# Where the lists' padding rows are written: whole regions early, or 128 rows behind each list's end

## The chip, the cores and the metric

The kernel runs on one core of a Trainium2 chip. A core has a matrix engine (TensorE, PE in the profile), a vector engine (VectorE, DVE), a scalar engine (ScalarE, ACT), GpSimd (POOL) and a sync engine (SP), each with its own in-order instruction stream; they meet through semaphores. Sixteen DMA engines move data between DRAM and the on-chip memory (SBUF). The DMAs of this kernel are issued by the sync engine, two small ones by ScalarE, and the scatters by GpSimd. The metric is the device time of one execution in microseconds, the median of several runs.

## What is computed

One block of a transformer on x of shape (4, 512, 512): a cross-attention whose output is added through a gate, and then a mixture of experts, added through a second gate. Both read x after a layer norm. Cut to what matters:

```python
x = x + tanh(g_xattn) * attention(layernorm(x), ctx, Wq, Wkv, Wout)   # 16 heads, 64 keys, causal
xf = layernorm(x).reshape(2048, 512)
scores = softmax(xf @ gate_w.T)                  # 8 experts
weights, idx = top_k(scores, 2)                  # two experts for every token
g = silu(xf @ w1[e].T) * (xf @ w3[e].T)          # every expert e, 512 -> 256
eo[e] = g @ w2[e].T                              # 256 -> 512
y = sum over the token's two experts of weight * eo[e]
z = silu(xf @ ws1.T) * (xf @ ws3.T) @ ws2.T      # a shared expert, for every token
out = x + tanh(g_ffn) * (y + z)
```

All is in float32. An expert sees only the tokens that chose it.

## The kernel before

**Stages.** The four batches go through attention one after another (`attention()`, L631). In the turn of batch b, TensorE also does what is left of batch b - 1: its output projection, the second layer norm's transposes, the gate product (`gate`, L378), the sum of the gate's parts (L390), and `choose` (L408), which picks two experts for each token on VectorE. The turn after that has `route` (L451) for that batch: two small products (L455 and L458) give each token its rank in its expert's list, `places()` turns ranks into row numbers on VectorE, and `scatter(t)` has GpSimd write 128 rows by an indirect DMA (L474), two for each of four tiles. The last batch has its own function, `last_routing` (L790), in which products of the shared expert (L622) fill TensorE's time.

**The lists.** `xg_d` is a tensor in DRAM with a region for each of eight experts, `CAP` = 2048 rows each, and a tail of seven tiles of 128 rows. A row is 528 floats: 512 of the token, and 16 that say where its result goes and with which weights. A list is filled from the start of its region. The experts' products read it in tiles of 128 rows, and the last tile of a list is only partly filled; a row that no token wrote must hold zeros and the number of a spare result row. So the kernel writes such a row (`zeros`, in SBUF, L249) over all of `xg_d` at the start: eight DMAs of 16 tiles and one of seven, L251 to L256, on the sync engine's queue, behind the loads of the inputs. A tenth DMA (L257) clears the results `y_d`. The first scatter waits for all nine.

`zeros` is the end of the tile `gs_sb`, into which the shared expert's products of the last batch are written late in the kernel; so those writes wait for every DMA that reads `zeros`.

**GpSimd's stream.** Its order is written by hand. In each turn it scales the softmax (`softmax`, L338, two instructions), then runs the eight scatters of `route`, prepares the tails of the rows (L510, L511), and scales the second half of the softmax. TensorE transposes that second half (L345) behind the gate product.

**After the last batch.** `tile_table` (L527) counts each list with one product (L530), and VectorE makes from the counts the row, the expert and the rank of each of up to 39 tiles (`row_of`, `expert_of`, `rank_of`, L544 to L581). Then comes the loop over tiles: `fetch(j)` (L858) on the sync engine reads the row number into a register (L862), and issues four DMAs of 64 KB (L864) and one small one (L870); VectorE transposes the tile in blocks (L885); TensorE multiplies by w1 and w3 (L897), by an identity (L916) and by w2 (L924); GpSimd adds the result into `y_d` by two indirect DMAs (L931). Fetches run four tiles ahead. In the end `y_d` is read back, added to the shared expert's output (L958) and to x, and stored.

**Who sets the order.** From L826 the order of TensorE, GpSimd, VectorE and ScalarE follows the program text by hand; the sync engine's is set by a scheduler with its own estimate of the times. Its queue before has, in this order: input loads, the nine fills, the clearing of `y_d`, the shared expert's weights (L588), w1 and w3 of all experts (L832), w2 of all experts (L839, eight loads), and the fetches. The first two blocked transposes of fetched tiles (L947) lie outside the hand-written part, so the scheduler places them on VectorE.

Of the kernel before, what the change touches and what calls it, by code (L numbers as in the profile page):

```python
# [14 lines left out]
I32 = mybir.dt.int32  # L15
AF = mybir.ActivationFunctionType
ALU = mybir.AluOpType
AX = mybir.AxisListType

P = 128  # L20
B, S, D = 4, 512, 512
SK, L = 64, 128
NH, HD = 16, 32
NE, FF = 8, 256
DC = D // P
QT = S // P
NT = B * QT
# [2 lines left out]
NPAIR = NH // 2  # L30
TOPK = 2
CAP = B * S

MAXT = (TOPK * B * S + NE * (P - 1)) // P
MINT = TOPK * B * S // P
ROWS = NE * CAP + (MAXT - TOPK * B * S // P) * P


META = 16
ROW = D + META  # L40
# [7 lines left out]
def gated_cross_attention_moe(  # L48
# [14 lines left out]
    nc = tc.nc  # L63
    const = ctx.enter_context(tc.tile_pool(name="const", bufs=1))
# [13 lines left out]
    zeros = gs_sb[:, B * FC * S - ROW :].unsqueeze(1)  # L78
# [16 lines left out]
    xg_d = dram.tile([ROWS, ROW], F32, name="xg_d")  # L95
    y_d = dram.tile([2 * (B * S + P), YH], F32, name="y_d")
    y_rows = y_d.rearrange("(r h) d -> r (h d)", h=2)
    xg_w = dram_disjoint_views(xg_d, TOPK * NT)
    y_w = dram_disjoint_views(y_d, 2)

    ident = const.tile([P, P], F32, name="ident")
# [6 lines left out]
    for c in range(1, DC):  # L108
# [4 lines left out]
        out=before, in_=ones, compare_op=ALU.is_gt, fill=0.0,  # L113
# [5 lines left out]
    for j in range(2):  # L119
# [8 lines left out]
        out=mask[:, 0, 0, :], in_=mask[:, 0, 0, :], compare_op=ALU.is_ge, fill=NEG,  # L128
# [5 lines left out]
    def counting(name, shape, pattern, base=0):  # L134
        n = int(np.prod(shape))
        i = const.tile([P, n], I32, name=f"{name}_i")
        nc.gpsimd.iota(i, pattern=pattern, base=base, channel_multiplier=0)
        f = const.tile([P, *shape], F32, name=name)
        counts.append((f.rearrange("p a b -> p (a b)"), i))
        return f  # L140
# [5 lines left out]
        channel_multiplier=2,  # L146
    )
    rank = counting("rank", [1, NE], [[-1, NE]], base=NE)
    region = counting("region", [1, NE], [[CAP, NE]])
    tile_start = counting("tile_start", [1, CAP // P], [[P, CAP // P]])  # L150
    tile_no = counting("tile_no", [MAXT, 1], [[1, MAXT]])

# [60 lines left out]
    with ExitStack() as attn:  # L213
# [22 lines left out]
        for b in range(1, B):  # L236
            nc.sync.dma_start(
                out=xs[b], in_=x[ts(b, S), :].rearrange("(t p) d -> p t d", p=P)
            )

        for g in range(HC):
            for j in range(2):
                nc.sync.dma_start(
                    out=wo_sb[ts(g, HD), j::2, :], in_=wo[ts(2 * (g % 2) + j, HD), g // 2 :: 2, :]
# [3 lines left out]

        nc.gpsimd.memset(zeros, 0.0)  # L249
        nc.gpsimd.tensor_copy(zeros[:, 0, D : D + 2].bitcast(I32), token[:, NT, :])  # L250
        for lo in range(0, ROWS, CAP):  # L251
            n = min(CAP, ROWS - lo) // P
            nc.sync.dma_start(  # L253
                out=xg_d[lo : lo + n * P, :].rearrange("(n p) d -> p n d", p=P),
                in_=zeros.broadcast_to([P, n, ROW]),
            )  # L256
        nc.sync.dma_start(  # L257
            out=y_rows.rearrange("(n p) d -> p n d", p=P),
            in_=zeros[:, :, 0:D].broadcast_to([P, NT + 1, D]),
# [191 lines left out]
        def route(b, xn, des, hot, hot2, both, earlier):  # L451

            pr = ps_mm.tile(full, F32, tag="mm", name="pr")
            flat = "p t e -> p (t e)"
            nc.tensor.matmul(  # L455
                pr.rearrange(flat), before, both.rearrange(flat), start=True, stop=False
            )
            nc.tensor.matmul(  # L458
                pr.rearrange(flat), ones, earlier.rearrange(flat), start=False, stop=True
            )  # L460

            def places():
                place = wide("place")
                nc.vector.tensor_tensor(place, pr, region.broadcast_to(full), ALU.add)
                for k, h in enumerate((hot, hot2)):
                    at = wide(f"at{k}")
                    nc.vector.tensor_tensor(at, place, h, ALU.mult)
                    where = row(at, ALU.add, f"where{k}")
                    nc.vector.tensor_copy(pos[b][:, :, k : k + 1], where)

            def scatter(t):
                nc.gpsimd.tensor_copy(xn[t][:, D + 2 : D + 5], des[:, t, :])
                for k in range(TOPK):
                    nc.gpsimd.indirect_dma_start(  # L474
                        out=xg_w[TOPK * (b * QT + t) + k],
                        out_offset=IndirectOffsetOnAxis(ap=pos[b][:, t, k : k + 1], axis=0),
                        in_=xn[t], in_offset=None,
                    )

            return places, scatter  # L480
# [43 lines left out]
                [xr.tile([P, ROW], F32, tag="xn2", name="xn2", bufs=QT) for t in range(QT)], b  # L524
            )

        def tile_table():  # L527

            pn = ps_mm.tile([P, 1, NE], F32, tag="mm", name="pn")
            nc.tensor.matmul(pn[:, 0, :], ones, taken[B], start=True, stop=True)  # L530
            n = small.tile([P, NE, 1], F32, tag="n", name="n")
            nc.vector.tensor_copy(n[:, :, 0], pn[:, 0, :])

            def table(shape, name):
                return const.tile([P, *shape], F32, name=name)

            def summed(src, shape, name):
                r = table(shape, name)
                nc.vector.tensor_reduce(r, src, AX.X, ALU.add)
                return r  # L540

            full = [P, NE, CAP // P]
            starts = table(full[1:], "starts")
            nc.vector.tensor_tensor(  # L544
                starts, n.broadcast_to(full), tile_start.broadcast_to(full), ALU.is_gt
            )
            tiles = table([1, NE], "tiles")
            nc.vector.tensor_reduce(tiles[:, 0, :], starts, AX.X, ALU.add)
            ends = table([1, NE], "ends")
            nc.vector.tensor_copy(ends, tiles)  # L550
            for e in range(1, NE):
                nc.vector.tensor_tensor(
                    ends[:, :, e : e + 1], ends[:, :, e - 1 : e], tiles[:, :, e : e + 1], ALU.add
                )
            full = [P, MAXT, NE]
            over = table(full[1:], "over")
            nc.vector.tensor_tensor(
                over, ends.broadcast_to(full), tile_no.broadcast_to(full), ALU.is_le
            )
            expert = summed(over, [MAXT, 1], "expert")  # L560
            nc.vector.tensor_tensor(over, over, tiles.broadcast_to(full), ALU.mult)
            first = summed(over, [MAXT, 1], "first")
            rows = table([MAXT, 1], "rows")
            nc.vector.tensor_tensor(rows, tile_no, first, ALU.subtract)
            nc.vector.tensor_scalar(rows, rows, float(P), None, ALU.mult)
            nc.vector.scalar_tensor_tensor(rows, expert, float(CAP), rows, ALU.mult, ALU.add)
            row_of = const.tile([P, MAXT], I32, name="row_of")
            nc.vector.tensor_copy(row_of, rows[:, :, 0])
            nc.vector.tensor_scalar(expert, expert, float(NE - 1), None, ALU.min)
            expert_of = const.tile([P, MAXT], I32, name="expert_of")  # L570
            nc.vector.tensor_copy(expert_of, expert[:, :, 0])


            rank_of = const.tile([P, MAXT], F32, name="rank_of")
            nc.vector.tensor_scalar(
                rank_of, expert[:, :, 0], -1.0, float(NE), ALU.mult, ALU.add
            )


            more = const.tile([P, 1], I32, name="more")  # L580
            nc.vector.tensor_scalar(more, ends[:, 0, NE - 1 :], -float(MINT), None, ALU.add)  # L581
            return row_of, expert_of, rank_of, more
# [207 lines left out]
        def last_routing(at, chosen, parts):  # L790
            ps_f = ending.enter_context(tc.tile_pool(name="ps_f", bufs=2, space=PSUM))
            filling = shared_in_turn(parts, ps_f)

            def fill(n):
                for _ in range(n):
                    next(filling)

            def scatter_all(places, scatter):
                places()
                for t in range(QT):  # L800
                    scatter(t)

            b = B - 1
            xn2 = addressed([rows_sb[:, ts(t, ROW)] for t in range(QT)], b)
            mv, rstd = new_stats()
            for t in range(QT):
                project_out(b, at, t)
                if not t:
                    scatter_all(*route(b - 1, *chosen))
                moments(b, mv, t)  # L810
            deviation(mv, rstd)()
            second_rows_of(xn2, b, mv, rstd)
            fill(5)
            turn(xn2, x2t[b])
            fill(1)
            scored = gate(b)
            fill(1)
            chosen = choose(b, gate_sum(scored))
            fill(6)
            scatter_all(*route(b, xn2, *chosen))  # L820
            table = tile_table()
            for _ in filling:
                pass
            return table
# [278 lines left out]
```

## Time and profile before

| | us |
|---|---|
| median of 3 runs | 469.99 (467.15 to 470.5) |
| profiled execution, its own time | 469.66 |
| its span | 467.9 |
| TensorE busy | 452.7 (97%) |
| VectorE busy | 253.1 (54%) |
| GpSimd busy | 178.9 (38%) |
| ScalarE busy | 131.1 (28%) |

98.10 MB go through the DMA engines, of which 62.71 MB are written to DRAM; the nine fills of `xg_d` are eight of 4224 KB and one of 1848 KB.

How to read it: a busy time is a sum over stages with different limits, and a share near 100% doesn't say that all of it is useful. "L338" is line 338 of the kernel. "pr<-pr,rs" is what an instruction writes and what it reads. "SPq" and "POOLq" are the instruction queues of the sync engine and GpSimd. The clock of TensorE (PEclk) is what the chip grants, as a share of full speed. A time in the trace is counted from the start of the span.

### The profile page before, as it was taken

What the parts mean: (1) busy time and instruction counts of PE and PEld (TensorE: products, weight loads), DVE (VectorE), ACT (ScalarE), POOL (GpSimd) and SP (SyncE); (2) the same over time, 40 slices, a digit from 0 to 9 for tenths busy, and PEclk for the clock granted to TensorE, in tenths of its full rate; (3) what the DMA queues carried; (4) which work ended last, traced back from release to release, by engine and by line L of the source; (5) the groups of instructions that cost most, each with busy time, mean ns of one, the idle gap of its engine ahead of it and who ended that gap; (6) DMA issues with size and microseconds to landing.
All of it is one profiled execution on the core that took longest, in us unless ns stands there. A gap on an engine that the chain in (4) does not pass through costs nothing.

```text
span 467.9 us, 6177 instructions
## 1 busy us (share of the span) xinstructions
PE 452.7 (97%) x1718; PEld 232.7 (50%) x1718; DVE 253.1 (54%) x604; ACT 131.1 (28%) x245; POOL 178.9 (38%) x188
## 2 busy tenths in 40 slices
PE   6999999999989999999999999999999999999994
PEld 5875555564646465454444444444444444444332
DVE  5659698779905975656421344333343333342485
ACT  3357642762533255413011111111111111111000
POOL 3003321303280374251600555565556565555400
PEclk9999999999997999999999999999999999999998
DMA  8989999999992040799835575666665666544498
GB/s 264 317 305 385 387 385 387 386 387 385 400 340 55 1 164 23 272 406 418 352 75 130 106 122 91 98 101 107 95 101 91 97 105 105 79 50 51 55 376 335
DMA packets 70783, 98.10 MB, mean 210 GB/s; under 512 B 11728, under 2 KB 40144, under 8 KB 69584
## 3 DMA queue, kind: packets, MB, share of 16 engines
q1 hardware_dynamic: 58096, 80.01, 50.9%
q0 software_dynamic: 12352, 17.57, 20.8%
q8 instruction: 17, 0.28, 0.3%
q14 instruction: 30, 0.25, 0.2%
q10 hardware_dynamic: 288, 0.00, 0.0%
HBM read 34.84 MB, written 62.71 MB: 208 GB/s over the span
## 4 chain that ended last, share of the span: by engine, by line
PE 65%; SPq 17%; DMA 7%; issue 4%; DVE 3%; POOL 2%; ACT 0%; DVEq 0%; POOLq 0%
PE ph L897 25%; SPq L253 16%; PE py L924 12%; PE ph L622 6%; PE pd L370 6%; PE ph L596 4%; DMA xg_d<-gs_sb 4%; PE pz L958 3%; DMA wo_sb<-in_wo_dram 2%; POOL xg_d L474 2%; PE pg L916 2%; PE early L596 1%; DVE yk L1028 1%; PE po L359 1%; DVE yk L1047 1%
## 5 line engine op out<-in xcount | busy, mean ns | idle before, releaser
L931 POOL DMA_INDIRECT y_d<-y,meta x68 | 105.6, 1553 | 103.2 <-DVE y L928 60.8
L897 PE MATMUL ph<-w_all,xgt 128*128 x272 | 122.5, 593 | 0.1
L897 PEld LDWEIGHTS ph<-w_all,xgt 128*128 128x128 f32 x272 | 49.1, 190 | 49.6 <-issue 49.5
L338 POOL TENSOR_TENSOR pr<-pr,rs 128x1024 f32<-128x1024 f32 x16 | 30.3, 1903 | 110.5 <-DVE rs L337 94.7
L924 PE MATMUL py<-w_all,gt 128*128 x136 | 63.9, 592 | 0.0
L908 DVE SCALAR_TENSOR_TENSOR g<-sl,w,ph 128x256 f32<-128x256 f32 x34 | 16.3, 481 | 87.4 <-ACT sl L906 87.4
L292 PE MATMUL pq<-xt,wq_sb 128*128 128x512 f32 (+1 forms) x160 | 56.9, 511 | 2.5 <-ACT xt L198 1.6
L370 PE MATMUL pd<-wo_sb,at 128*128 128x512 f32 x128 | 56.1, 595 | 0.0
L906 ACT ACTIVATE sl<-ph 128x256 f32<-128x256 f32 x34 | 13.1, 384 | 109.0 <-PE ph L897 109.0
L292 PEld LDWEIGHTS pq<-xt,wq_sb 128*128 128x128 f32 x160 | 29.7, 190 | 26.4 <-issue 20.1
L924 PEld LDWEIGHTS py<-w_all,gt 128*128 128x128 f32 x136 | 25.8, 190 | 32.5 <-issue 32.5
L928 DVE COPY y<-py 128x512 f32<-128x512 f32 x34 | 23.5, 692 | 27.8 <-PE py L924 27.8
L370 PEld LDWEIGHTS pd<-wo_sb,at 128*128 128x128 f32 x128 | 23.9, 190 | 29.1 <-issue 27.7
L958 PE MATMUL pz<-sh,gs_sb 128*128 128x512 f32 (+1 forms) x68 | 28.1, 570 | 1.4 <-DVE y L928 0.9
L622 PE MATMUL ph<-x2t,sh 128*128 128x512 f32 x64 | 28.6, 596 | 0.0
L918 ACT COPY gt<-pg 128x256 f32<-128x256 f32 x34 | 12.7, 373 | 53.1 <-PE pg L916 53.1
L155 DVE BATCH_NORM_STATS2 st<-x 128x6 f32<-128x512 f32 x32 | 21.8, 680 | 5.6 <-DMA x<-in_x_dram 5.1
L885 DVE STREAM_TRANSPOSE xgt<-xg 128x512 f32<-128x512 f32 x34 | 23.9, 702 | 1.0 <-DMA xg<-xg_d 1.0
L474 POOL DMA_INDIRECT xg_d<-xn,pos x16 | 15.9, 992 | 15.8 <-issue 14.1
L958 PEld LDWEIGHTS pz<-sh,gs_sb 128*128 128x128 f32 x68 | 12.7, 190 | 16.6 <-issue 15.1
L330 ACT ACTIVATE pr<-pr 128x1024 f32<-128x1024 f32 x16 | 16.9, 1058 | 14.2 <-DVE pr L329 11.5
L335 DVE TENSOR_REDUCE sm<-pr 128x16 f32<-128x1024 f32 x16 | 19.1, 1194 | 1.2 <-ACT pr L330 1.2
(167 smaller groups left out, 498.7 us busy)
## 6 DMA issues: line engine op xcount, KB each, us to landing
xg_d<-gs_sb SPq DMA_DIRECT2D x8, 4224.0 KB, 31.4
xg<-xg_d SPq DMA_DIRECT2D x144, 64.0 KB, 2.4
w_all<-in_w_dram SPq DMA_DIRECT2D x8, 1024.0 KB, 15.8
y_d<-gs_sb SPq DMA_DIRECT2D x1, 4352.0 KB, 31.6
w_all<-in_w_dram SPq DMA_DIRECT2D x8, 512.0 KB, 15.9
yk<-y_d SPq DMA_DIRECT2D x8, 512.0 KB, 6.5
out_dram<-yk SPq DMA_DIRECT2D x15, 256.0 KB, 5.1
x<-in_x_dram SPq DMA_DIRECT2D x3, 1024.0 KB, 11.3
```

The source lines that it names most:

```text
L253: nc.sync.dma_start(out=xg_d[lo : lo + n * P, :].rearrange("(n p) d -> p n d", p=P), in_=zeros.broadcast_to([P, n, ROW]),)
L292: nc.tensor.matmul(pq, wq_sb[:, k, ts(c, P)], xt[:, k, tokens], start=(k == 0), stop=(k == DC - 1),)
L338: nc.gpsimd.tensor_tensor(pr, pr, rs.broadcast_to([P, NH, SK]), ALU.mult)
L370: nc.tensor.matmul(pd, at[:, c, ts(t, P)], wo_sb[:, c, :], start=(c == 0), stop=(c == DC - 1),)
L474: nc.gpsimd.indirect_dma_start(out=xg_w[TOPK * (b * QT + t) + k], out_offset=IndirectOffsetOnAxis(ap=pos[b][:, t, k : k + 1], axis=0), in_ ...
L622: nc.tensor.matmul(ph[:, w, :], sh13[:, w, k, ts(f, P)], x2t[b][:, k, :], start=(k == 0), stop=(k == DC - 1),)
L885: nc.vector.transpose(xgt.rearrange("p c t k -> p t c k"), xg.rearrange("p t (c i) -> p t c i", c=DC))
L897: nc.tensor.matmul(ph, xgt[:, k, :], w13_all[:, ds(e, 1), :, k, :], start=(k == 0), stop=(k == DC - 1),)
L924: nc.tensor.matmul(py, gt[:, f, :], w2_all[:, ds(e, 1), f, :], start=(f == 0), stop=(f == FC - 1))
L928: nc.vector.tensor_copy(y, py)
L931: nc.gpsimd.indirect_dma_start(out=y_w[h], out_offset=IndirectOffsetOnAxis(ap=goes[j][:, h : h + 1].bitcast(I32), axis=0), in_=y[:, ts(h, ...
L958: nc.tensor.matmul(pz, gs[b][:, f, ts(t, P)], sh2[:, f, columns], start=(f == 0), stop=(f == FC - 1),)
```

## The change

The regions get 128 rows more (`REGION` = 2048 + 128), and the eight large fills are left out; the tail's fill and the clearing of `y_d` stay. In `last_routing` the product that counts the lists and the copy of the counts (now `counted`) come before `places()`. A new function, `fill_ends`, adds the counts to the regions' starts on VectorE and, for each expert, reads the sum into a register of the sync engine and stores 128 rows of `zeros` from there on. `tile_table` takes the counts as an argument.

```diff
+REGION = CAP + P
-ROWS = NE * CAP + (MAXT - TOPK * B * S // P) * P
+ROWS = NE * REGION + (MAXT - TOPK * B * S // P) * P
...
-    xg_w = dram_disjoint_views(xg_d, TOPK * NT)
+    xg_w = dram_disjoint_views(xg_d, TOPK * NT + NE)
...
-    region = counting("region", [1, NE], [[CAP, NE]])
+    region = counting("region", [1, NE], [[REGION, NE]])
...
-        for lo in range(0, ROWS, CAP):
-            n = min(CAP, ROWS - lo) // P
-            nc.sync.dma_start(
-                out=xg_d[lo : lo + n * P, :].rearrange("(n p) d -> p n d", p=P),
-                in_=zeros.broadcast_to([P, n, ROW]),
-            )
+        n = ROWS // P - NE * REGION // P
+        nc.sync.dma_start(
+            out=xg_d[NE * REGION :, :].rearrange("(n p) d -> p n d", p=P),
+            in_=zeros.broadcast_to([P, n, ROW]),
+        )
...
-        def tile_table():
+        def counted():
             pn = ps_mm.tile([P, 1, NE], F32, tag="mm", name="pn")
             nc.tensor.matmul(pn[:, 0, :], ones, taken[B], start=True, stop=True)
             n = small.tile([P, NE, 1], F32, tag="n", name="n")
             nc.vector.tensor_copy(n[:, :, 0], pn[:, 0, :])
+            return n
+
+        def fill_ends(n):
+            end = const.tile([P, NE], I32, name="end")
+            nc.vector.tensor_tensor(end, n[:, :, 0], region[:, 0, :], ALU.add)
+            for e in range(NE):
+                r = nc.sync.value_load(end[0:1, e : e + 1], min_val=0, max_val=ROWS - P)
+                nc.sync.dma_start(
+                    out=xg_w[TOPK * NT + e][ds(r, P), :], in_=zeros[:, 0, :]
+                )
+
+        def tile_table(n):
...
-            nc.vector.scalar_tensor_tensor(rows, expert, float(CAP), rows, ALU.mult, ALU.add)
+            nc.vector.scalar_tensor_tensor(rows, expert, float(REGION), rows, ALU.mult, ALU.add)
...
-            scatter_all(*route(b, xn2, *chosen))
-            table = tile_table()
+            places, scatter = route(b, xn2, *chosen)
+            n = counted()
+            places()
+            fill_ends(n)
+            for t in range(QT):
+                scatter(t)
+            table = tile_table(n)
```

In the built kernel the order of TensorE, ScalarE and GpSimd is that of before. On the sync engine the eight register loads and stores of `fill_ends` stand behind the fourth load of w2 and ahead of the other four and of all fetches. VectorE has one instruction more, and the first blocked transpose of a fetched tile stands behind the shared expert's product of the last batch's second half (L614), ahead of which it stood.

## The prediction

> **What bounds the kernel now.** I read the page's slices first, because shares over the whole span hide stages. In this view each digit is the busy tenth of one fortieth of the span (11.7 us).
>
> ```profile
> PE   6999999999989999999999999999999999999994
> PEclk9999999999997999999999999999999999999998
> DMA  8989999999992040799835575666665666544498
> ```
>
> TensorE is the bound: full in every slice but the first, the last and the twelfth. The DMA engines are full too in the first twelve slices, and all of that is the fill of the experts' lists. A full DMA row beside a full PE row costs nothing by itself; the fill costs only where PE shows a hole. The one in mid-kernel is slice 12, and PEclk falls in slice 13. So the next view is the chain of waits around 100 to 140 us (start, length, what).
>
> ```profile
> 98.22 17.87 DMA xg_d<-gs_sb
> 116.09 8.82 issue
> ...
> 125.86 1.25 POOL xg_d L474
> ...
> 135.58 0.96 POOL xg_d L474
> ...
> 137.77 1.91 POOL pr L338
> ...
> 139.72 1.09 PE pp L345 x8
> ```
>
> The last fill was issued at 98.22 and by the page's DMA issues took 26.6 us to land: 124.8. POOL's first scatter (L474) had its operands at 116.1 and could go only then. Eight scatters follow, then the softmax scaling (L338), queued behind them on POOL, and TensorE's transposes (L345) wait for that. How much TensorE lost is read from its own timeline (start, length, instruction), the same sequence of the batch before above that of this one.
>
> ```profile
> 93.30 1.07 PE L382 MATMUL pg<-rows_sb,gate_sb 128*32 128x512 f32 x8
> 101.21 0.41 PE L455 MATMUL pr<-both,before 128*128 128x32 f32 x2
> 136.82 1.06 PE L382 MATMUL pg<-x2t,gate_sb 128*32 128x512 f32 x8
> 139.72 1.09 PE L345 MATMUL pp<-ident,pr 128*128 128x128 f32 x8 [1.84 <-POOL pr L338]
> 149.55 0.41 PE L455 MATMUL pr<-both,before 128*128 128x32 f32 x2
> ```
>
> From the gate product to the routing product: 101.21 - 93.30 = 7.91 us, and 149.55 - 136.82 = 12.73 us. The difference is 4.82 us, of which 1.84 is the hole. The table by stretches (columns: stretch, length, busy of PE, PEld, DVE, ACT and POOL, PEclk, DMA share, GB/s) tells the rest.
>
> ```profile
> 137.00:140.00 3.00, 1.16 (x11) 0.28 (x4) 0.00 (x0) 1.10 (x2) 2.84 (x7) 1.00 0.88 241
> 143.00:146.00 3.00, 3.00 (x28) 1.00 (x34) 2.51 (x16) 1.32 (x3) 0.00 (x0) 0.50 0.17 36
> ```
>
> After the hole TensorE runs at half clock; over 140 to 149 us the granted clock is 0.69, 0.50 and 0.68, which is 9 x (1 - 0.62) = 3.4 us of lost clock, near the 4.82 - 1.84 = 2.98 us by which the sequence is longer.
>
> **What the change removes.** Eight fills of 4224 KB, 34.6 MB. Nothing else in that time waits for them: from 30 us on, TensorE idles outside the hole only 0.86 us behind ScalarE's copies (L348, at 43) and 0.24 us at 97; the fills begin at 24.75, when its first starved 30 us are over. The wait on POOL is then only for the tail fill, issued where the first of the nine is now (24.75); alone it is 1.8 MB, landed long before 116. So the first scatter starts near 116.2 instead of 125.86. Eight take 136.55 - 125.86 = 10.7 us: done at 126.9, four pairs of small POOL operations to 128.1. The scaling then waits for VectorE's reciprocals (128.44 and 129.87) and ends at 128.4 + 2 x 1.9 = 132.3. TensorE wants it at 137.9, after its gate product: 5.6 us of cover. What is late next there: nothing, as with the batch before, whose clock stays at 1.00.
>
> The Trainium skill speaks against so much gain. Its page "TensorE: Matmul & The Clock Gate" (Part 1) says that the clock is halved after at least one idle window of about 3.4 us and restored after a busy one; a hole of 1.84 us should not do that, and the saving would be 1.84 us. The row decides: 0.50 in 143 to 146, and the same sequence without a hole takes 7.91 us at 1.00. Saving by the rule 1.8, by the row 4.8. I take 4.8. But the page also says that the window runs free, so whether a given execution meets the dip can vary; the runs before lie at 467.15, 469.99 and 470.5, and the lowest is 2.84 us under the median, about the price of the dip. That is an inference, and it goes into the range.
>
> **What it adds, and where it moves.** What matters is the order of the sync engine's queue: the eight new pairs (a register load from `end`, one 264 KB store) stand behind the first four w2 loads and ahead of the last four and of every list fetch (L864). TensorE's order is the same; VectorE gets one operation more (`end`), has the copy of the counts ahead of the places, and transposes the first fetched tile after the last shared product (L614) instead of before it. All times below are those of the trace before; everything shifts with TensorE by the 4.8 us.
>
> VectorE: two operations of 0.16 to 0.18 us; the first of them delays the scatter's addresses by 0.2 us. Both lie under TensorE's shared products (219 to 246 us). Cost 0.
>
> Sync engine: addresses are done at 220.81, so `end` at about 221.1. One fill is priced by the nearest row, the list fetches: from the last issue of one fetch (236.57 + 0.35) to the first of the next (237.77) is 0.85 us, the register load among it, and one more DMA issue is 0.32 to 0.35: 1.2 us. Eight: 9.6 us, to 230.7. Four w2 issues of 0.33 each and their gaps: 232.2. The fetch's own register load: 233.0. The fetch can't go before the last scatter has landed anyway, which before was at 234.38, its first issue. So the issue of the first fetch is not delayed by the fills while a fill costs under 1.4 us.
>
> Its data is. The lines of the sync queue and of the two consumers:
>
> ```profile
> 234.38 1.94 SPq L864 DMA_DIRECT2D xg<-xg_d  x4
> ...
> 238.28 0.71 DVE L885 STREAM_TRANSPOSE xgt<-xg 128x512 f32<-128x512 f32 x1 [1.00 <-DMA xg<-xg_d]
> 242.84 0.69 DVE L604 TENSOR_TENSOR gs_sb<-gs_sb,ph 128x512 f32<-128x512 f32 x1 [3.84 <-PE ph L596]
> ...
> 246.02 3.60 PE L897 MATMUL ph<-w_all,xgt 128*128 x8
> ```
>
> The transpose of tile 0 ends at 239.0 and TensorE reads it at 246.0: 7 us of slack. Here the second rule matters: "DMA: Bandwidth & Descriptors" (Queues, rings and completion order) says that each DMA engine takes the descriptors of the sync engine's row in order. The fetch would then stand behind the last four w2 loads, 2.1 MB, issued from 231. At the 406 to 418 GB/s that the page shows for slices 18 and 19 they take 5.1 us; with about 2 us before the first byte counts (a fetch lands 2.4 us after issue) they are in at 238.5, and tile 0 at about 240 instead of 237.3. By the fetch row alone it would be 238. Either way it is in before 242.8, when VectorE is busy with the shared product, now ahead of it. Tile 0 is transposed at 243.5 to 244.3, under 246.0. Slack 1.8 us for VectorE, some 5 us for the data. The fills read the zeros that the last shared expert's result overwrites; ScalarE writes there at 239.35, the fills are in by 234. Cost 0; without the cover it would be the whole delay plus a new dip of 3 us. The last w2 experts are needed after 256.7.
>
> More traffic in that stage: eight fills of 264 KB, 2.2 MB. Slice 20 (222 to 234) moves 352 GB/s x 11.7 us = 4.1 MB; eight scatters of 128 rows of 2112 bytes are 2.2 of it, so about 2 MB is the end of w2. The fills take the place of that, and w2's last four the emptier time after it (75 GB/s in slice 21). Cost 0.
>
> The tail fill is the same size; wider regions only change addresses. The first product of the tile loop (246.0) to the end is TensorE's own pace and the output's tail, which I leave alone.
>
> Sum: 469.66 (this execution: span 467.9 and 1.76 around it) - 4.82 = 464.8. The median of the runs lies 0.3 above the execution, so 465.0 is stated.
>
> **The rivals.**
> First, gain and no more than the hole: the half clock meets another short pause, or was absent in many runs before. Saving 1.84: 467.8. For it: the skill's rule, the 467.15. Against: the same sequence ran at 1.00 in the other batches.
>
> Second, the wait on `end` becomes the bound, slower: the sync engine works in order, so tile 0 lands at about 221.1 + 8c + 9.3 for a price c of a fill (9.3 from 230.7 to 240, above). TensorE stalls when that passes 245.3, so that the transpose ends after 246.0: from c = 1.9. A stall of 1.8 us with a new dip of 3 eats the gain, at c = 2.1; from c = 2.7 it is slower by over 1%. If each fill waited for the landing of the one before (0.85 + 2.4 = 3.25 us), tile 0 would come at 256.4, a stall of 11.1: 464.8 + 11.1 + 3 = 479. Against it: each fill is on another of eight semaphores, and the fetches, built alike, go at 0.85 + 0.5 per issue without such a wait.
>
> Third, nothing moves: POOL waits for the tail or y_d fill or another DMA just as long. 469.7. Against: the tail fill is now first in the queue and 90 us early.
>
> **How the numbers follow.** Forecast 0.64 (465.0, own range 463.3 to 466.5); hole only or a partly covered late wait 0.19 (466.5 to 468.5); nothing moves 0.07; late tile 0 eats the gain or more 0.10, most of it above 474.7. The range 463.3 to 470.0 leaves out about 0.1 at the top and some of the bottom. One per cent is 4.7 us (it is about what a measurement of this kernel can tell from no change): faster by more means under 465.3, so the forecast falls to a little over two thirds there and one third within. Faster 0.46, within 0.46, slower 0.08.
>
> **What would show it.** Right: POOL's first scatter near 116; no hole before L345 in the third batch; the sequence from gate to routing product near 7.9 us and clock 1.00; DMA near empty from 45 to 110 us; the eight fills within about 10 us from some 216; TensorE without a gap before the first L897. Wrong: fills 2 us apart or more, a gap before the first L897 with a clock dip behind it, or a dip elsewhere.

## The result

The changed kernel takes 466.54 us (median of 20 runs, 465.47 to 468.69) where the kernel before, run beside it 20 times, takes 469.06 (466.57 to 471.93): a ratio of 0.9947 with the interval [0.9928, 0.9966]. That is 2.5 us less, half of the forecast's 4.8, and within the 1% that the text called about what can be told from no change; the interval is clear of 1 all the same. Of the prediction's cases, the forecast's own range (463.3 to 466.5) just misses it and that of the first rival, "gain and no more than the hole" (466.5 to 468.5), just holds it; the whole stated range (463.3 to 470.0) holds it too.

The profiled execution of after took 468.26 us, span 466.5; it lies near the top of its kernel's range, so only stages of the two profiles are compared here, not their spans. Some lines of after have other numbers: L198, L609, L882, L903 and L915 are before's L197, L596, L864, L885 and L897. The page's slices of after, rows as in the prediction:

```profile
PE   8999999999999989999999999999999999999894
PEclk9999999999999999999999999999999999999999
DMA  8996000000413040899883777666656666544498
...
PE 84%; DMA 7%; DVE 6%; ACT 1%; issue 1%; SPq 0%; DVEq 0%
```

The DMA row is empty in slices 5 to 10, where the fills were, and PEclk has no 7 in slice 13. In the chain of waits (last line) TensorE's share is 84%; before it was 65%, with 17% on the sync engine's queue.

The stage for which the change was worth something, in the timelines of GpSimd and TensorE of after (start, length, instruction, and in brackets the idle time ahead of it and what ended it):

```profile
117.69 1.19 POOL L474 DMA_INDIRECT xg_d<-xn,pos  x1 [0.29 <-POOL xn L472]
...
130.07 3.76 POOL L338 TENSOR_TENSOR pr<-pr,rs 128x1024 f32<-128x1024 f32 x2 [0.28 <-PE pt L198]
138.12 1.07 PE L382 MATMUL pg<-x2t,gate_sb 128*32 128x512 f32 x8
146.04 0.41 PE L455 MATMUL pr<-both,before 128*128 128x32 f32 x2
162.40 7.13 PE L609 MATMUL ph<-rows_sb,sh 128*128 128x512 f32 x16
173.53 1.14 PE L198 MATMUL pt<-ident,xn 128*128 128x128 f32 x8 [1.37 <-ACT prt L348]
174.51 3.70 PE L609 MATMUL ph<-rows_sb,sh 128*128 128x512 f32 x8
```

The scaling of the softmax is done at 133.83, 5.3 us ahead of the transposes (L345) that follow the gate product, and from the gate to the routing product it takes 146.04 - 138.12 = 7.92 us instead of 12.73. The last three lines are of the fourth batch's turn. The wait in them is new against the first profile of before: at that turn's transposes TensorE waits 1.37 us for ScalarE.

The late stage, with the eight stores ahead of the fetches, from the timelines of the sync engine, VectorE and TensorE of after:

```profile
220.32 12.29 SPq L541 DMA_DIRECT2D xg_d<-gs_sb  x8
232.65 1.87 SPq L857 DMA_DIRECT2D w_all<-in_w_dram  x4
235.77 2.11 SPq L882 DMA_DIRECT2D xg<-xg_d  x4
...
241.08 0.69 DVE L617 TENSOR_TENSOR gs_sb<-gs_sb,ph 128x512 f32<-128x512 f32 x1 [5.55 <-DMA xg<-xg_d]
243.37 0.71 DVE L903 STREAM_TRANSPOSE xgt<-xg 128x512 f32<-128x512 f32 x1 [1.61 <-DMA xg<-xg_d]
244.25 3.60 PE L915 MATMUL ph<-w_all,xgt 128*128 x8
```

The transpose of tile 0 ends at 244.08, and TensorE, busy until then with the shared expert, reads it at 244.25. So the 7 us of slack have shrunk to 0.2 us, and TensorE has no gap.

So between these two profiles the sum is right where the prediction looked (4.8 us gone in the third turn, nothing paid late), and the measured gain is 2.5. Two questions follow: how large the loss was in the other executions of the kernel before, and where the wait of the fourth turn comes from.

### The profile page after: what moved, and what is told of

It reads as the page before. It is cut to its first block, busy times and chain, and to the rows that moved or that the text cites. A ratio compares the mean times of both kernels' runs of the same rounds, so it can differ in the third digit from the quotient of the medians.

```text
span 466.5 us, 6220 instructions
## 1 busy us (share of the span) xinstructions
PE 452.7 (97%) x1718; PEld 233.2 (50%) x1718; DVE 253.2 (54%) x605; ACT 131.2 (28%) x245; POOL 178.7 (38%) x188
## 4 chain that ended last, share of the span: by engine, by line
PE 84%; DMA 7%; DVE 6%; ACT 1%; issue 1%; SPq 0%; DVEq 0%
PE ph L915 24%; PE pd L370 12%; PE py L942 11%; PE pq L292 11%; PE ph L635 6%; DMA y_d<-y,meta 5%; PE ph L609 5%; PE psc L306 3%; PE pt L198 3%; PE pp L345 2%; DVE yk L1046 2%; PE po L359 2%; PE early L609 1%; PE pg L934 1%; DVE yk L1065 1%; DMA yk<-y_d 1%
## 5 line engine op out<-in xcount | busy, mean ns | idle before, releaser
L915 PE MATMUL ph<-w_all,xgt 128*128 x272 | 122.5, 593 | 0.1
L915 PEld LDWEIGHTS ph<-w_all,xgt 128*128 128x128 f32 x272 | 49.0, 190 | 49.8 <-issue 49.7
L903 DVE STREAM_TRANSPOSE xgt<-xg 128x512 f32<-128x512 f32 x34 | 23.9, 703 | 3.0 <-DMA xg<-xg_d 3.0
L329 DVE TENSOR_TENSOR pr<-psc,mx 128x1024 f32<-128x1024 f32 x16 | 19.5, 1219 | 0.4
```

Source lines behind the costliest of these rows:

```text
L903: nc.vector.transpose(xgt.rearrange("p c t k -> p t c k"), xg.rearrange("p t (c i) -> p t c i", c=DC))
L915: nc.tensor.matmul(ph, xgt[:, k, :], w13_all[:, ds(e, 1), :, k, :], start=(k == 0), stop=(k == DC - 1),)
```

## The experiments

| kernel | us, median (range, runs) | ratio to before beside it |
|---|---|---|
| a1: after again | 466.37 (465.54 to 468.9, 7) | 0.9959 [0.993, 0.9987] |
| a2: before, third turn's scatters behind the scaling | 468.13 (466.25 to 469.94, 22) | 0.9993 [0.9978, 1.0008] |
| a3: before, half of each region filled early | 466.31 (465.14 to 466.92, 8) | 0.9953 [0.9936, 0.997] |
| a4: a3's early fills and after's late stores | 466.67 (465.6 to 468.76, 11) | 0.9965 [0.9948, 0.9982] |
| c1: a3 without the fourth turn's scatters | 465.81 (465.01 to 466.04, 4) | 0.9915 [0.9887, 0.9942] |
| c2, c4: before, profiled twice more | 471.97 and 469.06 (single) | |
| c3: after with sixteen late stores | 478.15 (477.45 to 478.76, 4) | 1.0178 [1.0151, 1.0206] |
| d1: after, last pair of the fourth turn's scatters later | 465.06 (464.29 to 465.7, 5) | 0.9936 [0.9901, 0.997] |
| d2: after, all of the fourth turn's scatters later | 472.51 (472.09 to 473.66, 4) | 1.01 [1.0078, 1.0122] |
| d3: after once more | 466.45 (466.0 to 469.12, 20) | 0.9957 [0.9939, 0.9975] |

Three groups, each beside the kernel before on its chip: 468.13 us for the a's (35 runs), 469.48 for the c's (7), 468.87 for the d's (24).

### First group: is it the hole, and do the late stores cost anything?

Theory A is the prediction's: the gain is hole and dip of the third turn, the late stores are hidden. B has the late stores eat part of it, C has the fill traffic itself slow the kernel.

a1 is the kernel after, unchanged.

> The changed kernel itself, for a second profile beside the others. Theory A (the gain is the hole behind the first scatter and its clock dip, smaller on average than in the one profile; everything late is hidden): about 466.5 us (0.995 of before). Theory B (the late stores cost a share of the gain, since the first tile is transposed only 0.3 us before TensorE reads it): 466.5 too, and in the profile either a gap before the first product with w1 and w3 or a transpose less than 1 us ahead of it. Both: no hole at the third batch's transposes. Open question: whether the gap of 1.4 us at the transposes of the fourth batch's turn, seen in the first profile, comes again; if it is a chance event it is gone, if it belongs to the change it is there.

a2 leaves the fills as they were and takes only the wait off the scaling's way: in the third batch's turn GpSimd scales first and scatters then.

```diff
-                if b > 1:
+                if b > 2:
                     for t in range(QT):
                         scatter(t)
...
                 softmax(p2)
                 if more:
                     softmax(p3)
+                if b == 2:
+                    for t in range(QT):
+                        scatter(t)
```

> The kernel before, with all its early fills, but with the first batch's eight scatters put behind the scaling of the softmax on GpSimd, so that the scaling doesn't queue behind a scatter that waits for the fills. No late stores. Theory A: the whole gain of the change without it: 466.5 us, equal to the changed kernel within 0.5. Theory B (late stores cost about 1 us): 465.3 to 465.7, faster than the changed kernel. Rival C (the traffic of 34.6 MB itself slows other work): 468 or more, near the kernel before.

a3 keeps the early fills but fills only the first 1024 rows of each region, which is enough for the lists of this input and not for any input; there are no late stores.

```diff
-            n = min(CAP, ROWS - lo) // P
+            n = min(CAP // 2, ROWS - lo) // P
```

> The kernel before with the early fills cut to the first 1024 rows of each region (right only while no list is longer): the last one lands near 75 us, before the first scatter. No late stores, the order of all engines as before. Theory A: 466.5 us, equal to the changed kernel. Theory B: 465.3 to 465.7, equal to the kernel with the scaling first. Rival C: between the kernel with the scaling first and the changed one.

a4 has both, the half fills early and the stores late.

```diff
-        n = ROWS // P - NE * REGION // P
-        nc.sync.dma_start(
-            out=xg_d[NE * REGION :, :].rearrange("(n p) d -> p n d", p=P),
-            in_=zeros.broadcast_to([P, n, ROW]),
-        )
+        for lo in range(0, ROWS, REGION):
+            n = min(CAP // 2, ROWS - lo) // P
+            nc.sync.dma_start(
+                out=xg_d[lo : lo + n * P, :].rearrange("(n p) d -> p n d", p=P),
+                in_=zeros.broadcast_to([P, n, ROW]),
+            )
```

> The changed kernel, with the first 1024 rows of each region filled early as well, so that the late stores do what is done already. Its difference from the kernel with the half early fills alone is the price of the late stage. Theory A: 0, both at 466.5. Theory B: about 1 us, 466.5 against 465.5.

Measured: a1, a3 and a4 lie within 0.4 us of one another, at 466.3 to 466.7. a3 has no late stores and a1 has no early fills, so neither B (a3 would be ahead of a1) nor C (a4 would be behind a1) shows, and half of the fills do as well as none: it is enough that the last fill lands before the first scatter could go. In a3 the sequence from gate to routing product takes 144.78 - 136.87 = 7.91 us.

a2 missed its mark: the hole is gone and nothing is gained. Its 468.13 us are what C expected, but the timelines speak against C: TensorE reaches the third batch's gate product at 136.79 in a2 with all of the fills, at 136.87 in a3 with half of them and at 136.81 in d3 with none. What a2 loses, it loses behind that point:

```profile
136.79 1.07 PE L382 MATMUL pg<-x2t,gate_sb 128*32 128x512 f32 x8
137.79 1.09 PE L345 MATMUL pp<-ident,pr 128*128 128x128 f32 x8
...
141.38 1.09 PE L359 MATMUL po<-prt,vals 64*32 64x512 f32 x16 [0.77 <-issue]
142.81 1.09 PE L359 MATMUL po<-prt,vals 64*32 64x512 f32 x16 [0.34 <-issue]
143.83 2.53 PE L306 MATMUL psc<-kt,qt 64*128 64x128 f32 x32
146.29 0.41 PE L455 MATMUL pr<-both,before 128*128 128x32 f32 x2
```

No wait is left in front of L345, but the sequence takes 146.29 - 136.79 = 9.50 us: small stalls turn up ahead of the next short instructions, while the last of the scatters (132.8 to 143.5) run. That scatters beside TensorE's chain of short, waiting instructions might cost something themselves was in none of the three theories; for this turn it was not tested further, but it pointed to the fourth turn, where eight scatters end beside such a chain: a1 waits 0.81 us there, a3 0.82, a4 0.79, a2 0.58 and 0.82, and the first profile of before not at all. My first reading was that the time is given back there when the hole goes. The second group tests that.

### Second group: the size of the loss before, the fourth turn, and where the late stores break

c2 and c4 are the kernel before, unchanged, profiled again.

> The kernel before, profiled again. If the size of the hole and of the dip behind it depends on where the clock's windows fall in an execution, the sequence from the gate product to the routing product in the third batch takes something else than 12.73 us, between 7.91 + 1.84 = 9.75 (hole, no dip) and about 13; if it is fixed by the program, 12.7 again. The wait of about 1 us at the fourth turn is absent again if the hole before it is what takes it away, and there (0.8 us or more) if it is chance.

> The kernel before, profiled once more, for the same question as the profile ahead of it: a third size of the sequence from gate to routing product in the third batch if the dip depends on the execution (9.75 to 13 us), 12.7 if it does not; at the fourth turn no wait if the hole takes it away.

TensorE's timeline in c2:

```profile
136.77 1.06 PE L382 MATMUL pg<-x2t,gate_sb 128*32 128x512 f32 x8
140.11 1.18 PE L345 MATMUL pp<-ident,pr 128*128 128x128 f32 x8 [2.28 <-POOL pr L338]
149.99 0.41 PE L455 MATMUL pr<-both,before 128*128 128x32 f32 x2
...
177.42 1.15 PE L197 MATMUL pt<-ident,xn 128*128 128x128 f32 x8 [0.86 <-ACT prt L348]
```

Its table by stretches, columns as in the prediction (the clock is the figure ahead of the DMA share):

```profile
143.00:146.00 3.00, 3.00 (x24) 1.65 (x30) 2.56 (x16) 1.17 (x2) 0.00 (x0) 0.50 0.22 40
```

The same timeline in c4:

```profile
136.81 1.06 PE L382 MATMUL pg<-x2t,gate_sb 128*32 128x512 f32 x8
139.39 1.09 PE L345 MATMUL pp<-ident,pr 128*128 128x128 f32 x8 [1.52 <-POOL pr L338]
146.45 0.41 PE L455 MATMUL pr<-both,before 128*128 128x32 f32 x2
...
173.95 1.15 PE L197 MATMUL pt<-ident,xn 128*128 128x128 f32 x8 [1.39 <-ACT prt L348]
```

And the same stretch of c4, at full clock:

```profile
143.00:146.00 3.00, 3.00 (x58) 1.85 (x44) 1.96 (x13) 2.19 (x6) 0.00 (x0) 1.00 0.12 25
```

The hole is in all three profiles of before (1.84, 2.28, 1.52 us), the dip in two. With the dip the sequence takes 12.73 and 13.22 us, without it 146.45 - 136.81 = 9.64. So in c4 the hole costs 9.64 - 7.92 = 1.7 us, and the half clock behind it costs 12.73 - 7.92 - 1.84 = 3.0 us in the first profile and 13.22 - 7.92 - 2.28 = 3.0 in c2. And the wait of the fourth turn is there in c2 and c4, with the hole ahead of it: it is no price of the change. The first profile of before had been spared it: there the turn takes 176.38 - 165.91 = 10.47 us.

```profile
165.91 7.13 PE L596 MATMUL ph<-rows_sb,sh 128*128 128x512 f32 x16
174.63 1.91 PE L197 MATMUL pt<-ident,xn 128*128 128x128 f32 x16
176.38 3.60 PE L596 MATMUL ph<-rows_sb,sh 128*128 128x512 f32 x8
...
173.81 1.06 POOL L474 DMA_INDIRECT xg_d<-gs_sb,pos  x1 [0.30 <-issue]
```

The clock records in the traces say more about the dip. The clock changes in steps of 3.413 us: the half clock lasts 6.83 us in the first profile and in c2, two steps, and the full clock ahead of it 136.53 and 133.12 us, 40 and 39 steps. In both, the hole lies between two steps (137.70 and 141.11; 137.57 and 140.99), and the half clock begins at the second. In c4 a step, counted back from the end of its full clock, falls into the hole at 138.67 and leaves 0.80 us of it on one side and 0.72 on the other. But c4's hole is also the shortest, and another wait in that execution, of 1.67 us and ending at 11.20, lies between two steps and has full clock behind it. So the length of the hole and its place among the steps are not told apart by these three profiles.

How often the dip is met can be read from the mean granted clock of every execution. 66 runs of before and 47 of after have it on record (of before those beside the experiments, of after those of the result, a1 and d3):

| mean granted clock | before, median us (runs) | after, median us (runs) |
|---|---|---|
| 0.996 to 1.000 | 467.88 (44) | 466.40 (47) |
| 0.994 to 0.995 | 468.98 (9) | none |
| 0.990 to 0.993 | 471.19 (13) | none |

A dip of 6.83 us takes 3.4 us of clock, or 0.007 of the mean, so the last row is that of a whole dip and the middle one, by this estimate, that of about half of one. A low mean need not come from this hole, though: a2, which hasn't got it, has 3 of 22 runs between 0.992 and 0.995. The profile on which the prediction rests had 0.990. Against after's 466.40 the three rows are 1.5, 2.6 and 4.8 us longer, which by their counts is (44 x 1.5 + 9 x 2.6 + 13 x 4.8) / 66 = 2.3 us on average. Measured were 2.5 (the result), 1.8 (a1) and 2.4 (d3). These aren't independent: the runs of the table are those behind the three measured gains, but for before's in the first.

c1 is a3 with the second batch's scatters left out.

```diff
-                if b > 1:
+                if b == 2:
                     for t in range(QT):
                         scatter(t)
```

> The before kernel with half early fills, and the second batch's eight scatters, which go out in the fourth batch's turn, left out (those rows stay zero, so a quarter of the lists' content is missing). Theory A, the time given back at the fourth turn comes from the scatters running there: the wait for ScalarE's copy at the transposes of the score products (0.8 to 1.4 us in the four kernels without the hole) vanishes, from the first shared product of the third batch's turn to that of the fourth it takes about 10.5 us instead of 11.5, and the kernel takes some 1 us less than the half-early one: ratio about 0.993. Rival B, it is a stall of the copies or of TensorE's order that has nothing to do with the scatters: 11.5 us and a wait of 0.8 us stay, ratio about 0.995. By C, scatters hidden and nothing else, the late fetches start sooner but nothing changes at the end, since the last batch's scatters stay.

TensorE in the fourth turn of c1:

```profile
162.38 7.13 PE L596 MATMUL ph<-rows_sb,sh 128*128 128x512 f32 x16
169.35 1.91 PE L345 MATMUL pp<-ident,pr 128*128 128x128 f32 x16
171.10 1.91 PE L197 MATMUL pt<-ident,xn 128*128 128x128 f32 x16
172.84 3.60 PE L596 MATMUL ph<-rows_sb,sh 128*128 128x512 f32 x8
```

From the first shared products to the next: 172.84 - 162.38 = 10.46 us and no wait, against 12.11 in the profile of after, 11.53 in a1, a3's 11.53, 12.05 in c2 and 12.12 in c4. A holds over B: the wait belongs to the scatters that run there, or to GpSimd's small operations behind them (L510, L511), which move with them. The ratio, 0.9915, is lower than the 0.993 expected, but its interval holds that.

c3 doubles the late stores: behind each a second one with a register load of its own, on the 128 rows that follow.

```diff
-    xg_w = dram_disjoint_views(xg_d, TOPK * NT + NE)
+    xg_w = dram_disjoint_views(xg_d, TOPK * NT + 2 * NE)
...
                 nc.sync.dma_start(
                     out=xg_w[TOPK * NT + e][ds(r, P), :], in_=zeros[:, 0, :]
                 )
+                r = nc.sync.value_load(end[0:1, e : e + 1], min_val=0, max_val=ROWS - 2 * P)
+                nc.sync.dma_start(
+                    out=xg_w[TOPK * NT + NE + e][P:, :][ds(r, P), :], in_=zeros[:, 0, :]
+                )
```

> The kernel after with sixteen late stores instead of eight: behind each a second one, with its own register load, of zeros on the 128 rows that follow. Theory A, the late stores are hidden while the sync queue is through with them before tile 0 is due, and 16 x 1.54 us is 12.3 us more: the fetch of tile 0 is transposed about 12 us later, at some 256 instead of 244.1, TensorE waits about 11.5 to 12 us ahead of the first list product, with a dip of up to 3 us behind it: 478 to 482, ratio about 1.02 to 1.03. Rival B, the price of a store is set by the waits for the landed data and not by the queue, and doubling costs less than 5 us at the end: under 473, ratio under 1.01.

The timelines of the sync queue, VectorE and TensorE in c3:

```profile
218.97 0.38 SPq L541 DMA_DIRECT2D xg_d<-gs_sb  x1
...
240.28 1.88 SPq L861 DMA_DIRECT2D w_all<-in_w_dram  x4
243.41 2.08 SPq L886 DMA_DIRECT2D xg<-xg_d  x4
...
250.45 0.71 DVE L907 STREAM_TRANSPOSE xgt<-xg 128x512 f32<-128x512 f32 x1 [6.76 <-DMA xg<-xg_d]
...
251.26 6.05 PE L919 MATMUL ph<-w_all,xgt 128*128 x8 [8.19 <-issue]
```

Two stretches of c3, one in the wait and one behind it:

```profile
248.00:251.00 3.00, 0.00 (x0) 0.00 (x0) 0.55 (x1) 0.00 (x0) 0.00 (x0) 0.50 0.67 115
251.00:254.00 3.00, 2.74 (x4) 1.22 (x5) 1.13 (x4) 0.00 (x0) 0.00 (x0) 0.50 0.33 70
```

The stores and their loads take 240.28 - 218.97 = 21.3 us for sixteen, against 232.65 - 220.32 = 12.3 for eight: 9.0 us more, not the 12.3 expected, since the later ones cost 1.12 us each. Of the 9.0 us, TensorE waits 8.19. It comes back at half clock: the eight list products take 6.05 us instead of 3.60. The kernel takes 478.15 - 466.45 = 11.7 us more than after (d3's runs), of which 8.2 is the wait and 6.05 - 3.60 = 2.4 the clock. Of the other 1.1 us, 0.6 is how far the kernel before differs between the two groups (469.48 and 468.87); the rest is not explained. A's mechanism holds; the late stage is a cover that eight stores all but use up, and behind it the second rival's wait is real.

### Third group: the scatters of the fourth turn

Theory D says that the wait sits at the end of the row of scatters; E that any scatter beside the transposes costs as much. F, tried with d3, is the reading of the clocks above. d1 moves the last two of eight behind the scaling of p2, d2 all eight, both from the kernel after (p2 and p3 are the scores of the third and fourth of the batch's four tiles).

```diff
                 if b > 1:
-                    for t in range(QT):
+                    for t in range(QT if more else QT - 1):
                         scatter(t)
...
                 softmax(p2)
+                if b == B - 1:
+                    for t in range(QT - 1, QT):
+                        scatter(t)
```

> The kernel after with the last two of the eight scatters of the fourth turn behind the scaling of p2 on POOL. Theory D, the stall at the fourth turn sits at the end of the row of scatters, wherever that is: the transposes of the normalized rows go without the wait for ScalarE's copy, from one group of shared products to the next it takes 10.5 to 10.9 us instead of 11.5 to 12.1, the last pair runs under shared products that wait for nothing, and the kernel takes 0.5 to 1.5 us less than the kernel after beside it. Rival E, any scatter running beside the transposes costs them about as much: 11.5 us or more stay, or the wait turns up at a later place, and the time is that of the kernel after within 0.5 us.

d2 is the same with `range(QT if more else 0)` and `range(QT)`.

> The kernel after with all eight scatters of the fourth turn behind the scaling of p2 on POOL. D: no wait at the fourth turn's transposes, 10.5 us from one group of shared products to the next, and 0.5 to 1.5 us less than the kernel after beside it, if the scaling of p3, now some 11 us later on POOL (from 178.65 to about 186), is not awaited before that; if it is, a hole of several us and a dip, slower than the kernel after by 2 to 8 us. E: no gain, since the scatters meet the next transposes instead.

> The kernel after once more, to be compared on the same chip with the two kernels that move scatters of the fourth turn: ratio to the kernel before 0.993 to 0.997, 11.5 to 12.1 us in the fourth turn. Its mean granted clock from run to run within 0.996 to 1.000, that of the kernel before from 0.990 to 1.000, with the time following the clock: that is theory F, the half clock behind the hole is met in a part of the executions only, so that the gain is 1.7 us for the hole and a part of 3 us for the clock. Without F the clocks of both have the same spread.

The timelines of TensorE and GpSimd in d1:

```profile
161.04 7.13 PE L609 MATMUL ph<-rows_sb,sh 128*128 128x512 f32 x16
168.01 1.91 PE L345 MATMUL pp<-ident,pr 128*128 128x128 f32 x16
169.76 1.91 PE L198 MATMUL pt<-ident,xn 128*128 128x128 f32 x16
171.50 3.60 PE L609 MATMUL ph<-rows_sb,sh 128*128 128x512 f32 x8
...
166.68 0.96 POOL L474 DMA_INDIRECT xg_d<-gs_sb,pos  x1 [0.30 <-issue]
...
174.76 1.04 POOL L474 DMA_INDIRECT xg_d<-gs_sb,pos  x1 [0.28 <-POOL gs_sb L472]
```

No scatter runs between 167.6 and 174.8, the transposes lie in that gap, and the turn takes 171.50 - 161.04 = 10.46 us, as without any scatters (d3: 12.12). All five runs of d1 (464.29 to 465.7) are below all twenty of d3 (466.0 to 469.12); the medians differ by 1.4 us. So d1 beats both kernels. It doesn't part D from E, since none of its scatters touches these transposes. The first profile of before speaks against E, since there scatters ran beside the first sixteen transposes and nothing waited; but the row also ended among the transposes, at 174.87, so it doesn't bear D out as it was put. What sets it apart is when the row ends, counted from the turn's first shared product: 8.96 us there, 9.2 in c2, 9.4 in after, a1, a3, a4, c4 and d3, and 10.3 in a2, all of which wait. What holds ScalarE's copies up there stays open.

d2's fourth turn takes 10.46 us too, and the scatters then stand in the way of the scaling of p3, as GpSimd's and TensorE's timelines show:

```profile
185.28 1.91 POOL L338 TENSOR_TENSOR pr<-pr,rs 128x1024 f32<-128x1024 f32 x1
187.25 1.97 PE L345 MATMUL pp<-ident,pr 128*128 128x128 f32 x8 [5.78 <-POOL rows_sb L510]
```

Its stretches in the wait and behind it:

```profile
184.00:187.00 3.00, 0.00 (x0) 0.00 (x0) 0.51 (x4) 0.00 (x0) 2.68 (x2) 0.50 0.46 183
...
190.00:193.00 3.00, 3.00 (x33) 0.70 (x18) 0.00 (x0) 1.18 (x3) 0.00 (x0) 0.50 0.01 3
```

A wait of 5.78 us in front of L345, and half clock behind it: 6.1 us more than d3. It is the hole of the kernel before once more, one turn later and larger.

F is borne out by d3 and its neighbours: the mean clock of d3's twenty runs lies within 0.996 and 1.000, that of the 24 runs of before within 0.990 and 1.000, the eight at 0.993 or less taking 470.4 to 471.5 us and the fifteen at 0.997 or more 466.8 to 469.6.

## Why the prediction was right or wrong

**The bound and the hole** were right. After's first scatter starts at 117.69; its turn is 1.3 us later than in the first profile (the first products, at 6.9 us, ran at half clock in that execution and took 3.75 us instead of 1.97), and 116.2 + 1.3 = 117.5. The scaling was to end at 132.3 + 1.3 = 133.6 and ended at 133.83. The sequence from gate to routing product is 7.92 us at full clock, as the batch before had it.

**"Saving by the rule 1.8, by the row 4.8. I take 4.8."** This is the term that was mis-sized. The row was one execution, and the page "TensorE: Matmul & The Clock Gate" of the Trainium skill (Part 1), which would have given 1.84 us, was nearer to most of them: in c4 a hole of 1.52 us left the clock at 1.00, and two thirds of the runs of before (44 of 66) have a mean clock like after's. It isn't right for all: holes of 1.84 and 2.28 us, shorter than its window of 3.4 us, were followed by 0.50. The clock's steps of 3.413 us in the traces agree with that window, but that it runs free, which the prediction put into its range only, doesn't explain a dip behind a hole that fills no window wherever it starts; whether the hole's length or its place decides stays open. What the runs show is how often: 13 of 66 have the mean clock of a whole dip and 9 that of about half of one, and the saving is 2.3 us on average, not 4.8. The argument that one of three runs was 2.84 us below the median was the evidence for it, and it was given too little weight.

**"What is late next there: nothing"** holds for the third turn. In the fourth, the sum was made against an execution that lacked the 1.0 to 1.7 us which the scatters cost there in the two other profiles of before and in all of after. So the profile of before had one loss more than most (the dip) and one less. Its sum of 464.8 is the time of a kernel with neither loss, and d1, which has neither, takes 465.06; with after's own 12.11 - 10.47 = 1.6 us put back it is 466.5 (465.9 with a1's 11.53), where 466.54 were measured. So as far as these sums go, the time was missed by the wait that the profile lacked, and the gain by the dip that most runs lack.

**VectorE** was right at 0.

**The sync engine** was right in the sign and wrong in both terms. A store with its register load took 12.3 / 8 = 1.54 us, not 1.2: 2.7 us in all. Tile 0 was to land 9.3 us behind the last store (230.7 to 240, by the ring order of "DMA: Bandwidth & Descriptors", Queues, rings and completion order); in the runs VectorE could start on it 10.8 us (after: 232.6 to 243.37), 10.1 (a1), 10.2 (c3) and 9.5 (d1) behind it. So the rule priced this step well, and the fetch row alone, 3.9 us from issue to transpose before against 243.37 - 235.77 = 7.6 in after, did not. VectorE's shared product was to hold the transpose up; in after it was done at 241.77 and the data came 1.6 us behind it. Of the 1.8 us of slack forecast for VectorE and some 5 for the data, 0.2 were left in the profiles of after and d3, 0.8 in a1's and 1.4 in d1's. "From c = 1.9" should have read about 1.6 to 1.7. The landing of tile 0 before was misread: VectorE's wait for it ends at 238.28, and 237.3 is where the wait begins. The cost was 0 all the same, as a3 against a4 bounds it (0.4 us, with overlapping intervals), and c3 shows the price behind the cover.

**A reading that was wrong and cost nothing.** The DMA engines are full in the first twelve slices, but not all of that is the fill of the lists: the fills begin at 24.75, and the loads of the inputs go ahead of them.

**The rivals.** The first is nearest to what most runs do, though its reason, a hole and no dip, leaves out the wait of the fourth turn. The second didn't occur, though it stood 0.2 us away; its 479 for a landing 11 us too late compares with c3's 478 for a wait of 8.2. The third fell: the wait for the fills is gone.

## What to carry to other kernels

A half clock that only some executions meet is to be weighed by how often it is met, not by the profile that shows it; the spread of the runs before tells how often, and a mean granted clock for each run tells it better. A profile of before can also lack a loss that most executions have, so a stage is read in more than one execution before its duration goes into a sum. And when indirect scatters end beside a chain of short instructions that wait for one another, moving a pair of them under long products can pay: here it is worth 1.4 us, more than half of the whole change.

## What was unexpected of the hardware

- Behind a hole of 1.84 or 2.28 us TensorE's clock was half for 6.83 us (3.4 us of clock lost), behind one of 1.52 us in the same place it wasn't. In every trace the clock changed in steps of 3.413 us.
- Eight indirect scatters of 128 rows, on GpSimd and on a queue that TensorE and ScalarE don't use, cost TensorE 1.0 to 1.7 us where the last of them ran beside transposes and copies that wait for one another (10.46 us without, 11.5 to 12.1 with), and nothing in one of three profiles of the kernel before, where they ended 0.2 to 0.5 us earlier.
- The price of a register load and a 264 KB store on the sync queue was not one number: up to 2.9 us while the scatters ran, 1.12 us after them (c3).
